# A warm-up on TensorE and a reordered prologue in a fused attention-times-FFN kernel

## The chip, the core and the metric

The kernel runs on one core of a Trainium2 chip. The metric is the device time of one execution in microseconds (us). Besides plain timed runs there is one profiled execution, from which all rows below come. The engines are TensorE (PE, with its weight loads as PEld), VectorE (DVE), ScalarE (ACT), GpSimd (POOL) and SyncE (SP), which here only issues DMA transfers; ACT's queue issues a few as well.

## The reference

The input is x of 4 sequences of 512 tokens with 512 features. A layer norm feeds two branches, and their product is added to x:

```
xn = layernorm(x)
q, k, v = split(xn @ w_qkv)              # 16 heads of 32
q, k = rope(rmsnorm(q) * q_gamma), rope(rmsnorm(k) * k_gamma)
s = softmax(causal(q k^T / sqrt(32))) v @ w_out
W = (wq - 128) * scale                   # three weights, given as int32
f = (silu(xn @ Wgate^T) * (xn @ Wup^T)) @ Wdown^T
out = x + s * silu(f)
```

The hidden width of the second branch is 1408, which is 11 blocks of 128.

## The kernel before

One function, `interleaved`, issues the whole program in an order written out by hand; each engine runs its own instructions in the order in which they are issued, and waits by semaphores for what it needs from others. The work goes by units (b, g): four sequences b, and in each four groups g of four heads. The tokens of one sequence are four tiles t of 128 rows. A unit has a hidden window (the hidden products of a chunk of the 11 blocks) and an attention window, beside which the projection of the next unit runs. The change lies ahead of all of that, in `prologue`, which prepares unit (0, 0), and in the loads issued before it.

The steps of the prologue, with the lines at which the profile shows them:

- `load_x` (L134) fetches the four x tiles on SP's queue, 256 KB each. ACT's queue fetches the two gammas (L151) and the rope table `tab` (L153, 256 KB). Then `load_wqkv` (L159) fetches the part of w_qkv that group 0 needs, in four loads of 192 KB on SP's queue, and `load_weights` (L251) the int32 FFN weights, one block of 256 KB at a time. A DMA takes one of eight semaphores in turn, and waits until the earlier DMA on that one has landed.
- `Norm.stats` (L336, L337), `Norm.roots` (L322, L323, on POOL) and `Norm.apply` (L344) normalise tile t in place.
- `Norm.turn` (L352) transposes a tile with four TensorE transposes into a bank of `bank_t` (two banks in turn), and ACT copies it into `xnT` (L353).
- `Norm.cut` splits `xnT` into a rounded part `xh` (ACT, L358) and the rest `xl` (DVE here, L359). The hidden products (L615) read both, for all four tiles.
- `prepare_table` (L208, L211) multiplies the gammas into `tab` on DVE.
- `Projection.product(t)` (L376) gives q, k and v of tile t: four matmuls of 128 x 384, in float32 each of them two rows in the trace. They need tile t of `xnT` and the four wqkv loads.
- `Projection.rotate(t)`: square and keep on ACT (L386, L389), rotation with `tab` on DVE (L410, L413, L417), then POOL adds, takes the inverse root and scales (L418, L322, L323, L420). `Projection.turn` (L430) later transposes q and k of all four tiles.
- `cast_weights` (L258) narrows a block of FFN weights on ACT; `turn_weights` (L268) transposes two blocks, eight TensorE transposes, and DVE subtracts the zero point on the way out (L271). Four such blocks must be finished before the first two hidden products.
- `prepare_scales` (L202, L203) transposes the scales, which the first gate (L626) needs.

The identity `ident` is made on POOL first of all (masks.py:197 and 199).

Of the kernel before, what the change touches and what calls it, by code (L numbers as in the profile page):

```python
# [21 lines left out]
P = 128  # L22
# [3 lines left out]
NT = N // P  # L26
# [25 lines left out]
def interleaved(  # L52
# [27 lines left out]
    nc = tc.nc  # L80
# [24 lines left out]
    def bank_t(name):  # L105
        return ps_t.tile([P, 512], F32, tag="t", name=name)
# [37 lines left out]
    ident = const.tile([P, P], F32, name="ident")  # L144
# [5 lines left out]
    for i, g in enumerate((q_gamma, k_gamma)):  # L150
        nc.scalar.dma_start(gam[:, i, 0, :], g.partition_broadcast(P))  # L151
    tab = const.tile([P, NT, 2, 2, HD], F32, name="tab")
    nc.scalar.dma_start(tab, rope.rearrange("(t p) a c d -> p t a c d", p=P))  # L153

    wqkv = const.tile([P, NC, 3, NC, P], F32, name="wqkv")

    def load_wqkv(groups):
        for c in range(NC):
            nc.sync.dma_start(  # L159
                wqkv[:, c, :, groups, :],  # L160
                w_qkv[ts(c, P), :].rearrange("p (i g d) -> p i g d", i=3, g=NC)[:, :, groups, :],
            )

    load_wqkv(slice(0, 1))


    mask = const.tile([P, N], BF16, name="mask")
# [18 lines left out]
    def load_scales():  # L186
        srow = work("srow")
        at = 0
        for s in (s_gate, s_up):
            n = s.shape[0] // P  # L190
            nc.sync.dma_start(srow[at : at + n, 0:P], s.rearrange("(c p) -> c p", p=P))
            at += n
        return srow, at
# [6 lines left out]
    def prepare_scales(srow, at):  # L200
        tp = bank_t("sps")
        nc.tensor.transpose(tp[:, 0:at], srow[0:at, 0:P], ident[0:at, 0:at])  # L202
        nc.vector.tensor_copy(scales, tp[:, 0:at])  # L203

    def prepare_table():

        for lo, hi in ((0, half), (half, 0)):
            nc.vector.tensor_copy(gam[:, :, 1, lo : lo + half], gam[:, :, 0, hi : hi + half])  # L208
        tab_f = tab.rearrange("p t a c d -> p t (a c d)")
        gam_f = gam.rearrange("p a c d -> p (a c d)")  # L210
        nc.vector.tensor_tensor(  # L211
            tab_f, tab_f, gam_f.unsqueeze(1).to_broadcast([P, NT, 4 * HD]), ALU.mult
        )
# [31 lines left out]
    def load_weights(n):  # L245
        for _ in range(n):
            if todo and rooms:
                src, k, dst, name = todo.pop(0)
                room = rooms.pop(0)
                raw = room[:, : k * P]  # L250
                nc.sync.dma_start(raw.bitcast(U32), src.bitcast(U32))  # L251
                loaded.append((now[0], room, raw, k, dst, name))

    def cast_weights():

        _, room, raw, k, dst, name = loaded.pop(0)
        narrow = raw.bitcast(BF16)[:, : k * P]
        nc.scalar.copy(narrow, raw.bitcast(U32))  # L258
        cast.append((now[0], room, narrow, k, dst, name))

    def turn_weights(n=2):


        bank = bank_t(f"wt_{len(finished)}").bitcast(BF16)
        blocks = [cast.pop(0) for _ in range(n)]
        for i, (_, room, narrow, k, _, _) in enumerate(blocks):
            for c in range(k):
                nc.tensor.transpose(bank[:, ts(i * 4 + c, P)], narrow[:, ts(c, P)], ident16)  # L268
        for i, (_, room, _, k, dst, name) in enumerate(blocks):
            at = len(finished)  # L270
            nc.vector.tensor_scalar(  # L271
                dst,
                bank[:, i * 4 * P : (i * 4 + k) * P].rearrange("p (c r) -> p c r", r=P),
                -ZERO_POINT,
                None,
                ALU.add,
                ALU.max,
                accum_out=largest[:, at : at + 1],
            )
            if at >= NC:  # L280
                rooms.append(room)
            finished.add(name)
# [722 lines left out]

    def prologue():
        norm, fresh = Norm(0), Projection(0, 0)
        load_weights(4)
        scales_in = load_scales()
        load_weights(4)  # L1010
        for t in range(NT):
            norm.stats(t)
            norm.roots(slice(t, t + 1))
            if t:
                norm.apply(t - 1)
                norm.turn(t - 1)
        norm.apply(NT - 1)
        prepare_table()
        norm.cut(0, nc.vector)
        norm.cut(1, nc.vector)  # L1020
        fresh.product(0)
        fresh.rotate(0)
        norm.turn(NT - 1)
        norm.cut(2, nc.vector)
        norm.cut(3, nc.vector)
        load_weights(3)
        for _ in range(4):
            cast_weights()
        fresh.product(1)
        fresh.rotate(1)  # L1030
        for _ in range(4):
            cast_weights()
        for t in range(2, NT):
            fresh.product(t)
            fresh.rotate(t)
            turn_weights()
        load_wqkv(slice(1, 2))
        now[0] += 1
        prepare_scales(*scales_in)
        return fresh  # L1040

    fresh, last, norm, done = prologue(), None, None, None
    for u, (b, g) in enumerate(units):
        result = Result(b - 1) if g == 0 and b else None
        done = result or done
        beside = [[], [], []]
        if g == NC - 2 and b + 1 < B:
            for t in range(NT):
                load_x(b + 1, t)
            norm = Norm(b + 1)  # L1050
# [23 lines left out]
        fresh = Projection(*units[u + 1])  # L1074
# [436 lines left out]
def attn_times_ffn(tc: tile.TileContext, *args: bass.AP):  # L1511

    nc = tc.nc
    with tc.tile_pool(name="flag", bufs=1) as flag:
        wide = flag.tile([1, 1], I32, name="wide")
        interleaved(tc, *args, wide=wide)
        over = nc.values_load(wide, min_val=0, max_val=1)
        with tc.If(over != 0):
            in_float32(tc, *args)
# [36 lines left out]
```

## Time and profile before

| what | us |
|---|---|
| three timed runs | 641.58, 640.67, 641.40 |
| their median | 641.4 |
| the profiled execution | 641.22 |
| its span, first to last instruction | 639.3 |

The span is what the profile shows; the 1.9 us between it and the profiled execution's time lie around it. Some places in the span:

| place | start, us |
|---|---|
| identity ready (POOL, masks.py:199) | 1.29 |
| first statistics of x (DVE L336), waits for x | 5.86 |
| first transposes of x (PE L352) | 8.39 |
| first product (PE L376) | 11.96 |
| second product (PE L376) | 16.30 |
| first hidden product (PE L615) | 25.79 |
| transposes of q and k (PE L430) | 33.85 |

In the timeline a row has its start, its length, engine, line, operation, written and read tiles, shapes and count; in brackets stands how long the engine had been idle and what ended that. Matmuls overlap in the pipeline, so rows of one engine may be longer than the distance between their starts. The clock column is the share of TensorE's full clock that was granted, as far as the profile recorded it.

### The profile page before, as it was taken

How to read it: one execution, taken by the hardware profiler on the slowest of the kernel's cores; microseconds unless marked ns; L12 is line 12 of the kernel's file. 1: busy time of each engine (PE TensorE's matmuls, PEld its weight loads, DVE VectorE, ACT ScalarE, POOL GpSimd, SP SyncE). 2: the span in 40 equal slices, each digit the busy share in tenths (PEclk: the TensorE clock that was granted, in tenths of full speed). 3: DMA queues.
4: the chain of work that ended last, by engine and by line, in shares of the span. 5: the costliest groups of instructions: out<-in, count | busy, mean ns of one | idle time of the engine just before them, and what ended most of it. 6: DMA issues, size and time to landing. Idle time of an engine off the chain costs nothing.

```text
span 639.3 us, 11822 instructions
## 1 busy us (share of the span) xinstructions
PE 614.7 (96%) x3918; PEld 407.0 (64%) x3918; DVE 491.5 (77%) x1265; ACT 336.8 (53%) x875; POOL 314.2 (49%) x360
## 2 busy tenths in 40 slices
PE   4999998999999999999999999999999999999995
PEld 2655765668665575767666576766766566676752
DVE  4667597897888479898798569799698767969553
ACT  2656574635756064555747145464748146464660
POOL 3824426354663834546473642638472561827422
PEclk9999998999999999999999999999999999999998
DMA  8342355343532436433234525533343506334502
GB/s 259 117 137 67 100 126 176 80 115 80 147 74 77 121 87 170 126 89 72 57 84 91 139 35 171 132 85 79 82 99 83 149 1 165 84 84 99 133 1 71
DMA packets 55408, 66.25 MB, mean 104 GB/s; under 512 B 7446, under 2 KB 36396, under 8 KB 55340
## 3 DMA queue, kind: packets, MB, share of 16 engines
q1 hardware_dynamic: 54380, 65.00, 39.6%
q8 instruction: 33, 0.54, 0.3%
q10 hardware_dynamic: 960, 0.43, 0.2%
q14 instruction: 35, 0.29, 0.1%
HBM read 24.42 MB, written 4.28 MB: 45 GB/s over the span
## 4 chain that ended last, share of the span: by engine, by line
PE 89%; DVE 5%; ACT 3%; DMA 1%; issue 1%; SPq 0%; DVEq 0%; ACTq 0%
PE h L615 25%; PE qkv L376 24%; PE so L708 9%; PE dn L662 7%; PE sc L460 7%; PE dn L645 6%; PE pv L547 6%; PE qkt L430 2%; ACT arena L491 1%; PE xnt L352 1%; PE wt L268 1%; DMA x<-in_L_attn_x 1%; PE pt L507 1%; DVE st L336 1%; DVE arena L529 1%
## 5 line engine op out<-in xcount | busy, mean ns | idle before, releaser
L376 PE MATMUL qkv<-wqkv,xnT 128*128 128x384 f32 x512 | 174.7, 494 | 3.0 <-DVE wuT L271 2.2
L491 ACT ACTIVATE arena<-arena,least 128x128 f32<-128x128 f32 (+3 forms) x256 | 140.5, 550 | 50.1 <-DVE least L481 49.7
L529 DVE STREAM_TRANSPOSE arena<-arena 128x512 f32<-128x512 f32 (+1 forms) x154 | 148.1, 1007 | 2.1 <-ACT arena L491 1.2
L376 PEld LDWEIGHTS qkv<-wqkv,xnT 128*128 128x128 f32 x512 | 97.1, 192 | 69.9 <-issue 4.9
L634 POOL TENSOR_TENSOR h<-sil,h 128x512 fp32r<-128x512 f32 x44 | 57.7, 1312 | 129.9 <-ACT h L633 129.9
L481 DVE CUSTOM_DVE_ANT_0 arena<-sc,mask 128x128 f32<-128x128 f32 (+3 forms) x256 | 109.1, 486 | 14.0 <-PE sc L460 13.3
L418 POOL TENSOR_TENSOR qk<-qk,qs 128x256 f32<-128x256 f32 x61 | 44.6, 731 | 137.4 <-DVE qs L413 136.0
L323 POOL TENSOR_TENSOR ss<-ss,minus_half 128x8 f32<-128x8 f32 x64 | 107.0, 1672 | 5.3
L386 ACT ACTIVATE squares<-qkv 128x256 f32<-128x256 f32 x64 | 24.4, 381 | 128.9 <-PE qkv L376 90.0
L632 DVE SCALAR_TENSOR_TENSOR sil<-h,scales,sil 128x512 f32<-128x512 f32 x44 | 32.8, 746 | 48.2 <-PE h L615 38.5
L633 ACT CAST h<-sil 128x512 fp32r<-128x512 f32 x44 | 27.3, 620 | 72.0 <-DVE sil L632 72.0
L708 PE MATMUL so<-wout,oT 128*128 128x512 f32 x128 | 58.1, 593 | 0.0
L410 DVE TENSOR_TENSOR qk<-qkv,tab 128x256 f32<-128x256 f32 x64 | 26.6, 415 | 34.3 <-ACT v L389 34.2
L662 PE MATMUL dn<-wdT,h 128*128 128x512 f32 x184 | 51.7, 414 | 0.5 <-DVE wdT L271 0.5
L615 PE MATMUL h<-xh,wuT 128*128 128x512 f32 x176 | 49.9, 405 | 2.2 <-ACT qT L126 2.2
L615 PE MATMUL h<-xh,wgT 128*128 128x512 f32 x176 | 50.1, 406 | 0.0
L460 PE MATMUL sc<-kT,qT 32*128 32x512 f32 (+3 forms) x512 | 49.3, 467 | 0.0
L662 PEld LDWEIGHTS dn<-wdT,h 128*128 128x128 f32 x184 | 32.0, 188 | 25.9 <-issue 16.9
L615 PE MATMUL h<-xl,wgT 128*128 128x512 f32 x176 | 48.2, 395 | 0.0
L615 PE MATMUL h<-xl,wuT 128*128 128x512 f32 x176 | 48.1, 395 | 0.0
L491 ACT ACTIVATION_READ_ACCUMULATOR arena<-arena,least 128x1 f32 x256 | 47.8, 187 | 0.0
L645 PE MATMUL dn<-wdT,h 128*128 128x512 f32 x168 | 43.9, 409 | 0.0
(93 smaller groups left out, 877.7 us busy)
## 6 DMA issues: line engine op xcount, KB each, us to landing
arena<-arena SPq DMA_DIRECT2D x56, 256.0 KB, 4.7
arena<-arena SPq DMA_DIRECT2D x56, 192.0 KB, 3.5
arena<-arena SPq DMA_DIRECT2D x56, 128.0 KB, 3.2
x<-in_L_attn_x SPq DMA_DIRECT2D x16, 256.0 KB, 3.8
out<-o SPq DMA_DIRECT2D x15, 256.0 KB, 2.5
arena<-arena SPq DMA_DIRECT2D x56, 64.0 KB, 2.1
wqkv<-in_L_attn_w_qkv SPq DMA_DIRECT2D x16, 192.0 KB, 4.8
xr<-in_L_attn_x SPq DMA_DIRECT2D x12, 256.0 KB, 3.9
```

Of the source, the lines that this page charges most:

```text
L323: nc.gpsimd.tensor_tensor(dst, dst, minus_half[:, : dst.shape[-1]], ALU.pow)
L376: nc.tensor.matmul(bank.rearrange("p (i d) -> p i d", i=3), lhsT=xnT[:, c, ts(t, P)], rhs=wqkv[:, c, :, self.g, :], start=(c == 0), stop=( ...
L418: adder.tensor_tensor(qk, qk, qs, ALU.add)
L460: nc.tensor.matmul(bank, lhsT=qT[rows, ts(self.t, P)], rhs=kT[rows, : self.keys], start=True, stop=True,)
L481: nc.vector.tensor_tensor_reduce(out=pr, in0=self.banks[j], in1=mask[:, N - self.keys :], scale=float(HD), scalar=3.0e38, op0=ALU.add, op1 ...
L491: nc.scalar.activation(pr, pr, AF.Exp, bias=least, scale=-1.0, accum_out=self.sums[:, j, self.t : self.t + 1],)
L529: nc.vector.transpose(way[:, :, blocks], probs[:, :, blocks])
L615: nc.tensor.matmul(bank, lhsT=w[:, c, ts(f, P)], rhs=a[:, c, :], start=(c == 0 and a is xh), stop=(c == NC - 1 and a is xl),)
L634: nc.gpsimd.tensor_tensor(to[:, 1, :], sil, to[:, 0, :].bitcast(F32), ALU.subtract)
L645: nc.tensor.matmul(bank, lhsT=h[:, f - fs[0], a, ts(t, P)], rhs=wdT[:, f, :], start=(f == fs[0] and a == 0), stop=(f == fs[-1] and a == 1),)
L662: nc.tensor.matmul(bank, lhsT=h[:, i, a, ts(t, P)], rhs=wdT[:, f, :], start=(i == 0 and a == 0), stop=(f == fs[-1] and a == 1),)
L708: nc.tensor.matmul(self.banks[t], lhsT=oT[:, g, ts(t, P)], rhs=wout[:, g, :], start=(g == 0), stop=(g == NC - 1),)
```

## The change

Three things are changed. TensorE transposes the identity onto itself 30 times into a bank of its own (`busy`) that nothing reads, before it works on x. The rope table's load moves from ACT's queue, where it was third, to SP's queue behind the four wqkv loads. And the prologue has another order: the product of tile 0 stands behind the transposes of tile 1 rather than behind those of tile 2, the products of tiles 1 and 2 behind the transposes of tiles 2 and 3; the four first weight casts stand ahead of the copy of tile 3 on ACT; the cuts of tiles 2 and 3 come after two more casts; and a pair of weight blocks is turned ahead of the rotation of tiles 2 and 3 rather than behind it. After the prologue nothing differs.

```diff
@@ loads
     tab = const.tile([P, NT, 2, 2, HD], F32, name="tab")
-    nc.scalar.dma_start(tab, rope.rearrange("(t p) a c d -> p t a c d", p=P))
...
     load_wqkv(slice(0, 1))
+    nc.sync.dma_start(tab, rope.rearrange("(t p) a c d -> p t a c d", p=P))
@@ def prologue():
         norm, fresh = Norm(0), Projection(0, 0)
+
+        busy = bank_t("busy")
+        for _ in range(30):
+            nc.tensor.transpose(busy[:, 0:P], ident, ident)
         load_weights(4)
         scales_in = load_scales()
         load_weights(4)
...
             norm.roots(slice(t, t + 1))
             if t:
                 norm.apply(t - 1)
+            if t in (1, 2):
                 norm.turn(t - 1)
         norm.apply(NT - 1)
+        fresh.product(0)
         prepare_table()
         norm.cut(0, nc.vector)
         norm.cut(1, nc.vector)
-        fresh.product(0)
         fresh.rotate(0)
-        norm.turn(NT - 1)
-        norm.cut(2, nc.vector)
-        norm.cut(3, nc.vector)
+        norm.turn(2)
+        fresh.product(1)
         load_weights(3)
         for _ in range(4):
             cast_weights()
-        fresh.product(1)
+        norm.turn(3)
         fresh.rotate(1)
-        for _ in range(4):
+        for _ in range(2):
             cast_weights()
+        norm.cut(2, nc.vector)
+        norm.cut(3, nc.vector)
         for t in range(2, NT):
             fresh.product(t)
+            turn_weights()
             fresh.rotate(t)
-            turn_weights()
+            if t == 2:
+                for _ in range(2):
+                    cast_weights()
```

## The prediction

> **What bounds the kernel now.** I read the page's first lines and its chain that ended last, then the chain of the first 50 us alone, the timeline of the same stretch, and the busy time in chosen windows.
>
> ```profile
> span 639.3 us, 11822 instructions
> ...
> PE 614.7 (96%) x3918; PEld 407.0 (64%) x3918; DVE 491.5 (77%) x1265; ACT 336.8 (53%) x875; POOL 314.2 (49%) x360
> ...
> PE 89%; DVE 5%; ACT 3%; DMA 1%; issue 1%; SPq 0%; DVEq 0%; ACTq 0%
> ```
>
> TensorE carries 89% of the chain. Whatever lets its stream begin earlier moves the whole kernel forward, as long as nothing behind the prologue absorbs it. The chain of the first 50 us (start, length, what):
>
> ```profile
> 1.17 5.68 DMA x<-in_L_attn_x
> ...
> 11.08 1.09 PE xnt L352 x4
> 12.17 3.86 PE qkv L376 x8
> 16.03 0.44 PE xnt L352 x4
> 16.46 5.16 PE qkv L376 x16
> ...
> 25.86 3.92 PE h L615 x16
> ...
> 34.02 0.89 PE qkt L430 x8
> ```
>
> From 11.08 on the chain is TensorE nearly without a break. The same work has two prices: four transposes of x (L352) 1.09 and then 0.44, one product (8 rows of L376) 3.86 and then 2.6. The timeline (start, length) has the same, and the two other rows that the sum needs:
>
> ```profile
> 9.07 0.55 DVE L344 TENSOR_SCALAR x<-x,mv,ln_rstd 128x512 f32<-128x512 f32 x1
> 9.68 1.12 PE L352 MATMUL xnt<-ident,x 128*128 128x128 f32 x4 [0.17 <-DVE x L344]
> ...
> 15.86 0.60 PE L352 MATMUL xnt<-ident,x 128*128 128x128 f32 x4
> ...
> 31.05 0.62 POOL L420 TENSOR_TENSOR qk<-qk,ss 128x256 f32<-128x256 f32 x1
> ```
>
> Windows of 2.54 us on L376 (columns: length, PE busy with rows, PEld busy with rows, clock, DMA):
>
> ```profile
> 11.96:14.50 2.54, 2.54 (x4) 1.35 (x5) 1.00 1.07 366
> 16.30:18.84 2.54, 2.54 (x8) 1.52 (x9) 1.00 1.01 353
> ```
>
> Four rows early, eight later: TensorE runs at half rate at first, though the clock column says 1.00 there. Later the column does show such a state:
>
> ```profile
> 7.79:11.20 3.41, 2.35 (x9) 1.00 1.17 315
> 11.20:14.62 3.42, 3.42 (x9) 1.00 1.06 368
> 35.10:38.51 3.41, 2.30 (x28) 1.00 0.41 121
> 96.54:99.95 3.41, 1.26 (x4) 1.00 0.90 213
> 99.95:103.36 3.41, 3.41 (x13) 0.50 0.50 181
> ```
>
> The 0.50 stretch is 3.41 us long. I cut the windows on that grid: 25 steps before it lies 14.62, which is where the rows of L376 shrink. Read so, a window decides the rate of the next: 3.42 of 3.42 busy released the clock, 2.35 (transposes alone) had not, 2.30 kept it, 1.26 lost it.
>
> **The warm-up (30 transposes).** Cold transposes start (1.12 - 0.42)/3 = 0.23 us apart at most (0.42 is one row's own length in the source view of L352), warm ones (0.60 - 0.27)/3 = 0.11. Their only wait is for the identity, on POOL, ready at 1.29. All cold they end at 1.4 + 30 x 0.22 = 8.0; released on the way, near 6.4. The first x tile is normalised at 7.79 + 0.55 = 8.34, so they hide in TensorE's empty 8.39 us and cost nothing. One full grid window fits inside, so the clock should be released between 4.8 and 8.2. Unknown: whether transposes count as activity at all (the 2.35 window had only those and did not release, but was no full window), and whether the gap of 0.5 to 2 us before x loses the clock again. I take released and kept, since a full window of unbroken work is nearer the 3.42 row than the 2.35 row. The other ends are rivals B and C.
>
> The Trainium skill, "TensorE: Matmul & The Clock Gate", section "What's actually happening", has a free-running window of 3413 ns, release after a busy one and throttling after an idle one. The trace has the 3.41 but lost the clock after a window with 1.26 us of work, so "idle" is wider than the page's word. By the page alone the gap before x would be harmless and the sum below would stand; by the row it may not be, which is B.
>
> **The order.** Tile 1 is ready at 9.07 + 0.55 = 9.63 as before (DVE and POOL do the same work in the same order), its transposes start at 9.68 and are issued by 10.12. Product 0 now needs only tile 0's copy, (8.99 + 0.6) = 9.6, and wqkv. The fourth wqkv load was issued at 7.31 and took 4.5 us to land: 11.8; its chunk is wanted at 10.12 + 6 x 0.32 = 12.05, margin 0.25, and the table's 256 KB no longer travel ahead of it. So TensorE runs unbroken from 10.12: product 0 (2.58, that is 8 x 0.323), xnt 2 (0.44), product 1 (2.58), xnt 3 (0.44), product 2 (2.58), weight turn (0.45), product 3 (2.58), weight turn (0.45): end 22.2. Before: 25.17. Then `sps` and `h` start at 22.4 against 25.86; the 0.48 of issue and the 0.21 of sps shrink to 0.2. Two h groups and a turn, 3.92 + 0.46 + 3.78, put qkt at 30.6 against 34.02: **3.4 us earlier**.
>
> What must keep up:
> - ACT. Copies of tiles 0 and 1 at 9.0 and 10.3, two xh casts until 12.1, square and keep of product 0 until 13.45, copy of tile 2 until 14.05 (wanted 15.7 at the latest), four weight casts at 0.52 apart until 16.2, copy of tile 3 until 16.95 (wanted at 19.2), square 1 and keep until 17.5, two casts, two xh casts until 19.6, product 2's square until 20.1, two casts until 21.1. Queued behind the four casts are the copy of tile 3 and product 1's square; the casts' loads land by 14.6 in the trace (issued 9.58, 4.8 to land), so nothing waits.
> - DVE. Table product at 12.46, xl 0 and 1 until 14.45, rotation 0 (1.15) then, against 16.64 before; rotation 1 at 17.5, xl 2 and 3 until 20.3, first weight pair 1.3, rotation 2, second pair, rotation 3 until 25.0, scales 25.2 against 27.92. ACT's table load of 1.28 follows, sil at 26.5, its gated product 27.2 against 30.01. All before qkt.
> - POOL. Each rotation takes 3.4 (rows 0.73, 0.24, 1.67, 0.62 and gaps; the first took 4.1). Four in series from 15.35 end at 29.6 against 31.67. qkt waits for this: slack 1.0, so POOL caps the gain at 4.3.
> - SP. The table's issue (0.46 on ACT's queue) now stands fifth after x, behind four wqkv loads and a wait for the k_gamma load (about 7.0), ahead of all weight loads. It delays each by at most one issue, 0.6 us; they are paced by landings, and the bytes before them are the same, so I book 0. Bounds of the landing: 11.85, where the same bytes end now, and 7.3 + 6.8 (its own time to land before) = 14.1. Wanted at 12.45. I take the near end, since only its order among the same bytes changes.
>
> After the prologue every engine's instructions are the same in the same order, so 3.4 carries to the end. Span 639.3 - 3.4 = 635.9, and with the 1.9 us around it (641.22 - 639.3) 637.8. The profiled run lies 0.2 under the median of 641.4, so **638.0**.
>
> **Rivals.**
> - B: released, then lost again in the gap. For a release at 4.8 to 7.5 the window after it holds 1.3 to 1.9 us of work, between the 1.26 that lost the clock and the 2.30 that kept it. Then 3.41 us at half rate lie from between 8.2 and 10.9: 0.9 to 1.7 of TensorE lost, gain about 1.9: **639.5**.
> - C: transposes don't count, the warm-up does nothing. Product 0 starts cold at 10.6 (tile 1's four at 0.22). With the release at 14.62 as now, 6.3 of 8 rows run cold, and each cold one costs 0.32: 2.0, and 0.45 for the transposes. Gain 3.4 - 2.45: **640.4**.
> - D: the table lands at 14.1. xl 0, xl 1 and rotation 0 wait behind its product, POOL ends 1.65 later, 31.25, and sets qkt: gain 2.7: **638.7**.
> - E, slower: all 30 transposes write the same 128 columns of one bank. If each waited for the one before to be written, they would go 0.42 apart and end at 1.4 + 12.6 = 14.0. Everything from tile 0 on would be 5.6 late at first; product 0 starts at 14.9 warm instead of 10.12: -3.4 + 4.8 = +1.4: **642.8**. It decides from 0.35 apart. Against it: product rows that add into one bank start 0.32 apart at 0.49 length.
>
> The stall at 96.5 that costs a half-rate window is in both kernels; whether it meets the grid badly is up to the grid's phase. 1.26 of lost work against none makes 1.7 us either way, and I count that in the range.
>
> **How the numbers follow.** Forecast 0.45, B 0.24, C 0.20, D 0.06, E 0.05. A measurement tells 0.2%, 1.3 us, from no change: the bound is 640.1. Forecast, D and nearly all of B are faster, C is mostly within it with a third below: faster 0.78, same 0.17, slower 0.05. The range takes in B and C and, below, most of the 1.7 from the stall: 636.5 to 640.6.
>
> **What would show it.** A row of 30 transposes that ends before 8.4, with their spacing halving on the way; L352's first four at 0.6; product 0 starting at 10.1 and 2.6 long; h at 22.4; qkt at 30.6; all later stages 3.4 earlier. Product rows of 0.85 length mean B or C; the spacing inside the 30 tells which. DVE idle before L211 means D. TensorE waiting before qkt for L420 means that POOL sets the end.

## The result and the profile after

| | before | changed |
|---|---|---|
| median of the timed runs, us | 641.03 (640.5 to 641.58, 4 runs) | 636.87 (636.26 to 637.52, 4 runs) |
| profiled execution, us | 641.22 | 637.45 |
| its span, us | 639.3 | 635.7 |
| first statistics of x (L336) | 5.86 | 5.50 |
| first product (L376) | 11.96 | 9.83 |
| first hidden product (L615) | 25.79 | 22.25 |
| transposes of q and k (L430) | 33.85 | 30.32 |

The ratio is 0.9935, with a 95% interval of 0.9922 to 0.9948: 4.2 us less, 0.65%. One run of the kernel before, beside the second group of experiments below, took 1569.72 us; it counts in that group's median of 640.80 (640.72 without it) and in no ratio. The changed kernel's page begins so:

```profile
span 635.7 us, 11880 instructions
...
PE 617.8 (97%) x3948; PEld 411.1 (65%) x3948; DVE 490.8 (77%) x1265; ACT 336.7 (53%) x875; POOL 314.2 (49%) x360
...
PE 87%; DVE 6%; ACT 4%; DMA 1%; issue 1%; POOL 0%; DVEq 0%; ACTq 0%
```

The chain of its first 50 us from the first TensorE piece on (start, length, what):

```profile
9.37 0.63 PE xnt L352 x4
10.00 2.58 PE qkv L376 x8
12.58 0.44 PE xnt L352 x4
13.02 2.58 PE qkv L376 x8
...
22.32 3.93 PE h L615 x16
...
30.48 0.89 PE qkt L430 x8
```

The first product now costs 2.58 like those behind it; before, it took 3.86, from 12.17 to 16.03. Four transposes cost 0.63 and then 0.44, against 1.09 and then 0.44 before. The timeline's TensorE rows have the warm-up:

```profile
1.34 6.00 PE L1011 MATMUL busy<-ident 128*128 128x128 f32 x30 [1.34 <-POOL ident masks.py:199]
8.03 0.66 PE L352 MATMUL xnt<-ident,x 128*128 128x128 f32 x4 [0.68 <-DVE x L344]
9.37 0.63 PE L352 MATMUL xnt<-ident,x 128*128 128x128 f32 x4 [0.69 <-DVE x L344]
9.83 2.75 PE L376 MATMUL qkv<-wqkv,xnT 128*128 128x384 f32 x8
```

The 30 end at 7.34, 0.7 before the first tile is there. `busy` is not a bank of its own but one of the two of `bank_t`, which tile 1's transposes take next; what those waited for is DVE (0.69), not the bank. Inside the group the starts are 0.213 apart, and from the 25th on 0.109, while one row's own length goes from 0.42 to 0.27: the clock is released at 6.53, by transposes alone. The windows on this execution's grid (columns: length, PE busy with rows, clock, DMA share, GB/s):

```profile
3.11:6.53 3.42, 3.42 (x18) 1.00 0.75 261
6.53:9.94 3.41, 2.04 (x16) 1.00 1.19 310
9.94:13.35 3.41, 3.41 (x15) 1.00 1.08 373
91.86:95.27 3.41, 1.21 (x7) 1.00 0.88 255
95.27:98.69 3.42, 3.42 (x7) 0.50 0.68 226
```

The window after the release holds 2.04 us of work, and the clock stays. Of the 2.04, 0.81 is the end of the 30 transposes (6.53 to 7.34), and the rest is the transposes of tiles 0 and 1 (0.66 and 0.57). The stall of the kernel before, now at 92.5, still costs this execution one window at half rate.

### The profile page after: what moved, and what is told of

It is laid out like the page before. It is cut to its first block, busy times and chain, and to the rows that moved or that the text cites. A ratio compares the mean times of both kernels' runs of the same rounds, so it can differ in the third digit from the quotient of the medians.

```text
span 635.7 us, 11880 instructions
## 1 busy us (share of the span) xinstructions
PE 617.8 (97%) x3948; PEld 411.1 (65%) x3948; DVE 490.8 (77%) x1265; ACT 336.7 (53%) x875; POOL 314.2 (49%) x360
## 4 chain that ended last, share of the span: by engine, by line
PE 87%; DVE 6%; ACT 4%; DMA 1%; issue 1%; POOL 0%; DVEq 0%; ACTq 0%
PE h L615 25%; PE qkv L376 24%; PE so L708 9%; PE dn L662 6%; PE sc L460 6%; PE dn L645 6%; PE pv L547 6%; ACT arena L491 2%; PE qkt L430 2%; PE xnt L352 1%; DVE arena L529 1%; PE wt L268 1%; DMA x<-in_L_attn_x 1%; PE pt L507 1%; DVE wuT L271 1%
## 5 line engine op out<-in xcount | busy, mean ns | idle before, releaser
L376 PE MATMUL qkv<-wqkv,xnT 128*128 128x384 f32 x512 | 173.8, 492 | 3.0 <-DVE wuT L271 2.2
L376 PEld LDWEIGHTS qkv<-wqkv,xnT 128*128 128x128 f32 x512 | 96.7, 192 | 69.3 <-issue 4.6
L615 PE MATMUL h<-xh,wuT 128*128 128x512 f32 x176 | 49.9, 405 | 1.9 <-ACT qT L126 1.9
L615 PE MATMUL h<-xh,wgT 128*128 128x512 f32 x176 | 50.2, 406 | 0.0
L615 PE MATMUL h<-xl,wgT 128*128 128x512 f32 x176 | 48.1, 395 | 0.0
L615 PE MATMUL h<-xl,wuT 128*128 128x512 f32 x176 | 48.1, 395 | 0.0
```

What stands on the lines that cost most here:

```text
L376: nc.tensor.matmul(bank.rearrange("p (i d) -> p i d", i=3), lhsT=xnT[:, c, ts(t, P)], rhs=wqkv[:, c, :, self.g, :], start=(c == 0), stop=( ...
L615: nc.tensor.matmul(bank, lhsT=w[:, c, ts(f, P)], rhs=a[:, c, :], start=(c == 0 and a is xh), stop=(c == NC - 1 and a is xl),)
```

## The experiments

All were timed beside the kernel before in three groups; its median was 640.77 beside the first four, 640.80 beside the next four and 641.17 beside the last three. Kernels of different groups are best compared by their ratios to the kernel before in their own group; a ratio need not be the quotient of the two medians.

| kernel | median, us | ratio to before (95%) | h starts | qkt starts |
|---|---|---|---|---|
| no warm-up | 638.27 | 0.9967 (0.9955 to 0.9979) | 23.84 | 31.92 |
| warm-up only | 639.43 | 0.9979 (0.9969 to 0.9989) | 25.59 | 33.66 |
| table only | 639.45 | 0.9983 (0.9974 to 0.9993) | 24.71 | 32.78 |
| order only | 638.71 | 0.9966 (0.9954 to 0.9978) | 23.72 | 31.80 |
| 15 transposes | 638.67 | 0.9968 (0.9956 to 0.9980) | 23.96 | 32.05 |
| 60 transposes | 638.54 | 0.9964 (0.9951 to 0.9977) | 23.65 | 31.72 |
| stall filled | 635.82 | 0.9927 (0.9914 to 0.9940) | 22.19 | 30.27 |
| changed kernel again | 636.08 | 0.9932 (0.9919 to 0.9945) | 22.11 | 30.18 |
| bank emptied first | 635.08 | 0.9906 (0.9892 to 0.9921) | 22.09 | 30.17 |
| turns behind rotations | 636.32 | 0.9935 (0.9921 to 0.9948) | 22.38 | 30.46 |
| table on ACT | 636.52 | 0.9937 (0.9925 to 0.9950) | 22.33 | 30.42 |

**The changed kernel without the warm-up.**

```diff
-        busy = bank_t("busy")
-        for _ in range(30):
-            nc.tensor.transpose(busy[:, 0:P], ident, ident)
```

> The changed kernel without the 30 transposes; order and table as changed. If the clock carries a part of the gain by itself: tile 1's transposes are issued by 10.2, product 0 runs rows of 0.85 until a full busy window has passed, 3 to 8 of its rows at 0.32 more each, and 0.45 for the transposes: 1.4 to 2.9 lost against the changed kernel, h (L615) at 23.8 to 25.2, time about 639.1. Rival: the order does it all and the cold rows hide behind DVE and POOL: h within 0.3 of 22.25 or qkt within 0.3 of 30.3, time below 637.4.

638.27, 2.2 over the changed kernel's second run (which stands in the next group). Its TensorE rows:

```profile
7.90 2.37 PE L352 MATMUL xnt<-ident,x 128*128 128x128 f32 x8 [7.90 <-DVE x L344]
10.06 4.12 PE L376 MATMUL qkv<-wqkv,xnT 128*128 128x384 f32 x8
```

Product 0 starts early but is cold: 4.12 against 2.75. The price reaches h (23.84 against 22.11) and qkt (31.92 against 30.18) undiminished, so nothing hides it: 1.7 in the traces. What the medians have above that, 0.5, stays open.

**The kernel before with the warm-up alone**: the three lines above added at the start of `prologue`.

> The kernel before plus the 30 transposes alone. If the clock is worth something without the order: product 0 stands behind tile 2's transposes (tile 2 is ready at 10.95), starts at 11.5 and takes 2.6 instead of 3.9; h at 23.4 to 23.8 against 25.8, time about 638.9. Rival: without the order another engine takes over (casts on ACT end at 20.2 and hold the first weight turn, rotation 3 holds the scales): gain under 1, time 640 or more.

In the profiled execution h gained 0.2 only, but not for the reason of the expectation's rival:

```profile
0.66:4.07 3.41, 2.73 (x13) 1.00 0.52 84
4.07:7.49 3.42, 2.08 (x19) 1.00 0.95 306
7.49:10.90 3.41, 1.29 (x8) 1.00 1.09 296
10.90:14.31 3.41, 3.32 (x8) 0.50 1.04 378
```

The clock was released at 4.07, after 2.73 us of transposes. Then the window 7.49 to 10.90 held two tiles' transposes and nothing else, 1.29, and the next one ran at half rate. It covers product 0 of the old order from its start at 11.86 to 14.31, and the product took 3.96. This is rival B of the prediction, seen in one execution, the slowest of eleven (641.09). Two other runs had its mean granted clock, 0.992, and took 640.90 and 641.00; the eight at 0.994 to 0.999 took 638.01 to 639.95. That fits: where the clock is lost again, nothing of the gain is left. The median gains 1.3.

**The table's load alone**: the kernel before with the load on SP's queue, behind `load_wqkv(slice(0, 1))`.

> The kernel before with the table's load on SP's queue behind the four wqkv loads. If the table's transfer delays x: first statistics (L336) at 5.5 instead of 5.86 and everything 0.36 earlier, time about 640.7. Rival: the earlier x in the changed kernel's trace is chance: first statistics at 5.8 or later, time as before.

First statistics at 5.40, and at 5.81 in the next experiment, which has the table on ACT's queue. The gain of the median, 1.3, is more than that and more than was expected; the reason stays open. The profiled execution gained 1.1 at h because it was also released at 12.93, against 14.62 in the profile of before, which is the grid and not the edit; but at 640.15 it is one of the slower of its eleven runs, so this doesn't explain the median.

**The order alone**: no warm-up, the table on ACT's queue.

> The new order alone: no transposes, the table on ACT's queue. If the three parts add up: the time without warm-up plus 0.36, about 639.5, product 0 starting at 10.5 with rows of 0.85. Rival: the order needs the warm clock to pay, because tile 2's transposes now also stand behind a cold product: no gain, 641.

638.71: 2.1 less than before, and qkt at 31.80 against 33.85. The order pays without the warm clock. This trace was released at 12.13, against 14.62 in the profile of before, so a part of its 2.05 at qkt is the grid; the gain rests on the median of six runs.

**15 and 60 transposes.**

```diff
-        for _ in range(30):
+        for _ in range(15):      # the other kernel: 60
```

> The changed kernel with 15 transposes instead of 30. All cold they end at 1.34 + 15 x 0.213 = 4.5. If a window of the 3.41 us grid releases the clock only when it holds between 2.4 and 2.7 us of work, and loses it below 1.3 to 1.6, about half of the executions are never released by the 15, and the others lose the clock again in the empty 3.5 us before x: product 0 cold, time like the kernel without warm-up, 638.3. Rival: any burst of work starts the clock and 15 do as well as 30: product rows of 0.49, time 636.9.

638.67, as without a warm-up: that there are transposes ahead of x is not enough. In the profile the 15 ended at 4.80:

```profile
2.86:6.27 3.41, 1.95 (x10) 1.00 0.81 265
6.27:9.68 3.41, 1.64 (x7) 1.00 1.12 310
9.68:13.10 3.42, 3.42 (x8) 1.00 1.05 361
```

No window before 9.68 holds enough, and the release comes at 13.10, after the first full window of real work.

> The changed kernel with 60 transposes. If they go at 0.213 cold and 0.109 warm with no wait between them, they end at 9.3 to 10.9, past tile 0 (8.03), and product 0 starts at 10.2 to 11.8 instead of 9.83; TensorE sets the end, so the same 0.4 to 2.0 come out at qkt and in the time: about 638.0. Rival: slack elsewhere hides it, time 636.9; or writes to one place go one after the other at 0.42, then they end past 14 and the time is 641 or more.

638.54, 2.5 over the changed kernel in the same group, so the whole gain of the warm-up is gone. The 60 ended at 10.03. Tile 0's transposes started at 9.86, against 7.89 in that run of the changed kernel, product 0 at 11.14 against 9.70, and h at 23.65 against 22.11: 1.4 to 1.5 of the 2.0 by which the warm-up holds up tile 0 reach product 0 and h. It also settles the spacing: 60 in 8.7 us, nowhere 0.42 apart.

**The stall filled.**

```diff
+                if t == NT - 1 and (b, g) == (0, 1):
+                    for _ in range(18):
+                        nc.tensor.transpose(fresh.spare, ident, ident)
                 fresh.product(t, other=t == NT - 1 ...
```

`fresh.spare` is the last 128 columns of product 0's bank, which the projection leaves unused; the lines that set it are left out here.

> The changed kernel with 18 more transposes of the identity in the stall of 2.4 us at 92.5, where product 3 waits for a bank that DVE empties. They write 128 unused columns of product 0's bank. If the stall is what loses the clock for one window, no half-rate window is left before the end of the span, and the executions that had one gain 1.7: median 1.0 to 1.7 under the changed kernel's in the same batch. Rival: the 18 (2.0 us) delay product 3 or the weights' turn, or the loss comes from elsewhere: same time or up to 0.5 slower.

635.82 against 636.08 in the same group: the difference is inside both intervals. The profiled execution had no half-rate window before the end, but neither had the changed kernel's in this group, whose stall fell across two windows. That the fill helps is not shown; that it does no harm beyond the noise is. The expected 1.0 to 1.7 did not come.

**The changed kernel again.**

> The changed kernel again, beside the other three. By the windows read so far it always keeps the clock through the prologue: tile 0 and 1 and the early product 0 put at least 1.7 us of work into every window after the release. Product 0 with rows of 0.49, h at 22.0 to 22.5, median 636.9, spread of the stall's window 1.7. Rival: it loses the clock in some executions as the transposes alone did: some times above 638.

636.08, from 635.61 to 637.38, h at 22.11 and product 0 warm. The upper rival did not occur.

**The weight bank emptied first.** The fill covers the stall; this edit shortens it.

```diff
+            if b == 0 and t == 1:
+                weights(1)
             if t == 1 and g:
                 add()
                 last.divide()
-            if b == 0 and t:
+            if b == 0 and t > 1:
                 weights(1)
```

> The changed kernel, but in the windows of sequence 0 DVE empties the weight bank (L271) before the sum and the division (L678, L593), not behind them. The stall at 92.4 waits for that L271: it would end 1.3 earlier, 1.1 us long. If TensorE sets the end there, 1.3 less and no half-rate window after a stall this short: 634.6 to 635.0. Rival: DVE runs without a break there and sets the end, so TensorE gets the bank sooner and waits later for the rotation: no change, 636.1.

635.08, the fastest of all and 1.0 under the changed kernel's second run, which stands in another group; the intervals of the two ratios barely overlap. The row that ends the stall, in the changed kernel's first and second profile and then here:

```profile
94.87 4.54 PE L376 MATMUL qkv<-wqkv,xnT 128*128 128x384 f32 x8 [2.20 <-DVE wuT L271]
```

```profile
94.73 2.85 PE L376 MATMUL qkv<-wqkv,xnT 128*128 128x384 f32 x8 [2.21 <-DVE wuT L271]
```

```profile
93.56 2.85 PE L376 MATMUL qkv<-wqkv,xnT 128*128 128x384 f32 x8 [1.05 <-DVE wuT L271]
```

TensorE waits 1.05 instead of 2.2, and the product starts 1.17 earlier than in the second profile, with h at the same place (22.09 and 22.11). Of that, 0.7 is left at the end of the span (633.1 against 633.8): TensorE sets the end there for the most part. The product runs at full rate, but in the second profile it did so without the edit, where the stall fell across two windows; that this edit keeps the clock in every execution is not shown.

**Turns behind the rotations again.**

```diff
             fresh.product(t)
-            turn_weights()
             fresh.rotate(t)
+            turn_weights()
```

> The changed kernel with the weight pairs turned behind the rotations of tiles 2 and 3 again. If the sooner weight passes are worth the 0.48 that TensorE idled before sps: DVE empties the first pair 1.2 later, sps and h wait for it until 22.6 instead of 22.15, qkt and everything behind 0.4 later, 636.5. Rival: slack covers it, h at 22.15 and the time as the changed kernel's 636.1; the products' order is then the whole of the order's gain.

h at 22.38, 0.28 later, because `sps` finds its bank emptied later. `bank_t` has two banks in turn, so `sps` takes that of the first weight pair; DVE has emptied it at 22.14 here and at 21.10 in the changed kernel again. (The row names the turn L268, the last thing on its engine, which had ended at 22.01.)

```profile
22.24 0.21 PE L202 MATMUL sps<-ident,srow 22*128 22x22 f32 x1 [0.23 <-PE wt L268]
```

The time, 636.32, can't tell that from nothing. So the place of the turns is worth 0.28 of the 2.05 that the order alone gained at qkt; how the products, the casts and the cuts share the rest was not taken apart.

**The table on ACT's queue in the changed kernel.**

> The changed kernel with the table's load on ACT's queue, ahead of the wqkv loads, as before. If the table's transfer is what delays x: first statistics at 5.8 instead of 5.3 to 5.5, everything 0.4 later, 636.5. Rival: it also pushes the wqkv loads or the table wait matters on DVE: product 0 more than 0.5 later, or DVE idle before L211.

Statistics at 5.44, hardly later than in the other kernels, but tile 1's transposes at 9.46 against 9.21 in the first kernel of the group, and product 0 at 9.93 against 9.68: 0.25. Of the expectation, the later first statistics did not come; the price fell on tile 1. The DMA queues between 5 and 7 us show why (q1 is SP's, q10 ACT's; packets, MB, share of the time of 16 DMA engines), in the kernel before and in the changed one:

```profile
q1 hardware_dynamic: 276, 0.50, 65.7%
q10 hardware_dynamic: 569, 0.24, 41.7%
```

```profile
q1 hardware_dynamic: 587, 0.75, 102.1%
q10 hardware_dynamic: 115, 0.01, 4.4%
```

With the table on ACT's queue its 256 KB move while the x tiles do, and SP's queue moves a third less. It is this move and not the rest of the change: SP's queue moves 0.75 MB with the table alone moved, and 0.46 here, with it moved back. In all four traces with the table on ACT's queue the slowest x tile lands 6.9 to 7.1 us after its issue, and tile 1's normalisation (L344) starts at 8.77 to 9.07. In the nine with it on SP's queue that is 5.5 to 5.8 and 8.49 to 8.71. The means of the two groups, 8.96 and 8.59, lie 0.4 apart.

## Why the prediction was right, point by point

- **What bounds**: right. TensorE from the first tile on; 3.5 at qkt came through as 3.6 in the span.
- **The warm-up**: right in kind. Transposes count (released at 6.53 and 4.07 by transposes alone), they go at 0.213 and 0.109 with no wait, and hide before x. The earliest release, 4.8 in the forecast, was set too late: a window needs no full 3.41 of work, 2.73 was enough. Without the transposes the changed kernel took 2.2 more.
- **Why the clock was kept**: the forecast took this as the likelier case without a reason from the order, so this part was luck. In the old order the same 30 transposes lost the clock in the profiled execution (rival B, the warm-up alone). In the new order all six traces with 30 transposes kept it: the window after the release held 1.80 to 2.35, mostly transposes, where B had reckoned with 1.3 to 1.9. What the order adds comes one window later. In the stretch in which the warm-up alone had 1.29, the changed kernel's rows have 2.19, since product 0 starts 2.0 us earlier (9.83 against 11.86):

```profile
7.49:10.90 3.41, 2.19 (x12) 1.00 1.18 304
```

  This stretch is not on that execution's own grid. But where the release came nearly as early as in the warm-up alone, at 4.62 (table on ACT) and 4.69 (bank emptied first), the second window after the release, 8.04 to 11.45 and 8.10 to 11.51, held 2.65 and 2.73, and the clock stayed. That the order protects the warm-up follows from these windows and one lost clock. The times don't show it: warm-up, table and order alone gained 1.3, 1.3 and 2.1, which add up to the 4.2 and 4.7 of the changed kernel.
- **The order**: right. Product 0 was forecast at 10.12 and came at 9.83, h at 22.4 and came at 22.25, qkt at 30.6 and came at 30.32; the 0.3 at product 0 is x's earlier start, tile 1's transposes at 9.37 against 9.68. The sooner weight passes were taken to save the 0.48 of issue and most of the 0.21 of sps; by themselves they are worth 0.28.
- **The table**: "the bytes before them are the same, so I book 0" was the step that failed. It looked at the weights behind the table and not at the x tiles ahead of it, which no longer share the DMA engines with the table (the queues above). So tile 1 was not ready "as before": its transposes came 0.3 earlier, and on the mean of all traces the move is worth 0.4 there, which the sum lacked.
- **The size**: 638.0 against 636.87, and 636.08 in the second group, which lies under the forecast's range. The sum was 3.4; against its own profile the change gave 641.22 - 637.45 = 3.8, and x's earlier start is about the difference. Why the medians differ by 4.2 and 4.7 stays open. The stall's window may be a part: the profiled execution of the changed kernel had it and is the second slowest of its ten runs, and over the 45 other runs of the kernel before, the 13 with a granted clock of 0.997 or more have a median of 640.19, the other 32 of 641.25. It isn't all, since at 0.996 the changed kernel took 636.28 in one run and 637.52 in another.
- **The rivals**: B took place, though in another kernel. C fell, since transposes release the clock. Its price for a warm-up that does nothing, 2.45, was near the 2.2 that its absence cost; its 640.4 lay above the 638.27 of that kernel mainly because the forecast under it was 1.1 to 1.9 too high. D fell: DVE went from L208 to L211 without idle time. E fell at 0.213.

By the Trainium skill, "TensorE: Matmul & The Clock Gate", section "What's actually happening", the window runs freely and the transition point varies with where the first matmul falls in it. The traces agree in kind: releases at 12.13, 12.82, 12.93 and 14.62 in kernels without a warm-up, and half-rate windows of 3.41 us. The four releases lie 2.5 us apart, more than the plus or minus 500 ns that the page gives.

## What to carry to other kernels

If the engine that bounds a kernel waits for its first input, let it do the same kind of work on whatever is there, long enough to fill one clock window wherever the grid falls, and ending before the input comes: 15 transposes bought nothing here, 60 ran over the input and gave the gain back, 30 fitted. Then see that real work follows closely enough, since a window with little work in it (1.3 of 3.41 us here) takes the clock away again, at the start as in a later stall. And when a load is moved, look at what it travelled beside as well as at what waits for it.

## What the runs showed of the hardware

In the windows read here, PE's busy time in a window of 3.41 us goes with the clock of the next, and the two states have different thresholds. From the cold state 2.73, 3.12, 3.27 and 3.41 released it, 1.38, 1.45, 1.64, 1.95, 2.28 and 2.35 did not. From the released state 1.17, 1.21, 1.22, 1.26, 1.29 and 1.31 lost it, 1.58, 1.63, 2.04, 2.08 and 2.30 kept it. Nothing was read between 2.35 and 2.73, nor between 1.31 and 1.58. The one at 1.63 is the stall of the kernel without warm-up, split by the grid; much the same stall of 2.2 to 2.3 us costs a window in some executions and nothing in others:

```profile
94.74:98.15 3.41, 1.63 (x5) 1.00 0.89 225
98.15:101.57 3.42, 3.42 (x20) 1.00 0.65 209
```

The clock column says 1.00 before the first release, where rows run at half rate; the rows, not the column, tell the cold start.
